# Ties between two queues: marks left by ScalarE instead of VectorE, and a fused mean subtraction in layernorm

## The chip, the cores and the metric

The kernel runs on one core of a Trainium2 chip. The metric is device time in microseconds. Three runs of the kernel before took 3631.34, 3631.67 and 3632.71 us; the median, 3631.67 us, is the time before. One more execution was taken with the hardware profiler on.

## The reference, cut to what matters

Sixteen graphs of 1024 nodes and 64 channels pass through four layers. Each layer starts with the same normalisation, and uses the adjacency matrix in its own way:

```python
def _layernorm(x, axis=-1, eps=1e-5):
    m = jnp.mean(x, axis=axis, keepdims=True)
    v = jnp.var(x, axis=axis, keepdims=True)
    return (x - m) / jnp.sqrt(v + eps)

# in each of the four layers
h = jnp.maximum(_layernorm(x, axis=-1), 0.0)
x = x + layer(h, adj)
```

- Layer 0 multiplies the adjacency with h (the messages), and puts h and the messages through two small matrices with a tanh between.
- Layer 1 is a weighted mean over neighbours: (A + I) h divided by the row sums.
- Layer 2 first drops some neighbours of nodes that have more than ten. For every node and channel it then sorts the values of the remaining neighbours and takes a weighted sum of their quartiles, which goes through two small matrices. This is where the gathers and sorts of the kernel come from.
- Layer 3 multiplies the adjacency with h once more, divides by the degree, and adds two small matrix products and a bias.

## The kernel before

**Engines and streams.** The kernel is one long program per engine, and each engine works through its own in order. The order is made when the program is written out. Six Python generators ("streams") each walk over the sixteen graphs: `adjacency` (load, transpose, which neighbours are dropped, keys), `layers` (layers 0 and 1 and the layernorm of layer 2), `tail` (the rest of layer 2, and layer 3), `gathers`, `neighbour_lists` and `sorts`. A loop at the end of `direct_path` always resumes the first stream in this list whose due time has come. Due times come from a small model, the object `clk`, with a planned time for VectorE (`clk.dve`), TensorE (`clk.pe`), ScalarE (`clk.act`) and GpSimd (`clk.pool`). A stream adds the planned cost of what it has issued, and yields the planned time at which it wants to go on. So a change of a planned cost can change the order of instructions, on VectorE above all.

`after(dve, pe, act, lat)` (line 824) is the helper with which a stream adds the planned costs of a step: VectorE's first, then TensorE's from there, then ScalarE's from there.

**Lists, gathers, sorts.** `neighbour_lists` finds each node's neighbours with repeated maxima over a row of keys (lines 1119 and 1133); the rows of keys are loaded by GpSimd with indirect transfers (line 1100, four buffers). Nodes are ordered by number of neighbours, and eight blocks of 128 nodes form five groups. For each group `gathers` has GpSimd issue one indirect transfer per neighbour place and block (line 1294: 124 of them per graph, 1984 in all), which fetch 128 rows of h into a buffer `raw`. Each group has one buffer, so its gathers for a graph follow its sort for the graph before. `sorts` runs a sorting network on VectorE (line 1327), then weighted sums (line 1346). The result is written out, and `tail` fetches it back in node order with eight more indirect transfers on GpSimd (line 1366). The planned cost of a gather is 1.39 us. A stretch of four gathers is issued when VectorE's planned time has come within 5 us of GpSimd's (`yield clk.pool - 5`).

**Ties.** At 35 places per graph (ahead of every stretch of gathers and once ahead of the key loads, 560 in all) the kernel calls `gate()` (line 920). If more than 3 us of VectorE's planned time have passed since the last one, VectorE writes one element of a tile `mark` (line 923; 8 slots in rotation, planned at 0.15 us), and GpSimd copies this element into a tile `gate` (line 925). The copied value is never used. The copy has to wait for VectorE's write, and everything behind it in GpSimd's order with it. The write of a slot has to wait for GpSimd's copy of eight marks before.

**Layernorm.** `preln` (line 849) runs four times per graph. VectorE sums each node's 64 channels (line 854), multiplies the sums by 1/64 (855), subtracts this from x by a broadcast (856); ScalarE squares (857); VectorE sums again (859); ScalarE takes the root (860); VectorE inverts and multiplies (862, 863); ScalarE applies the maximum with zero (864). In one of the four, x is read from PSUM.

**ScalarE around it.** In `layers`, TensorE's messages (line 883, 32 multiplications of 512 columns) are copied out by ScalarE (line 884). For layer 1, eight passes over the transposed adjacency follow on ScalarE, which give the degrees (line 1228). The step is accounted with

```python
        yield after(0, pe=14.0, act=1.1) + 6.0
        clk.act += 10
```

so that the planned time of the eight passes is added once the stream is resumed.

Of the kernel before, what the change touches and what calls it, by code (L numbers as in the profile page):

```python
# [7 lines left out]
F32 = mybir.dt.float32  # L8
# [6 lines left out]
ALU = mybir.AluOpType  # L15
AX = mybir.AxisListType

P = 128
C = 64
NB = 8  # L20
# [712 lines left out]
def direct_path(ctx: ExitStack, tc: tile.TileContext, t: dict, out: bass.AP, flag):  # L733
# [3 lines left out]
    nc = tc.nc  # L737
# [3 lines left out]
    const = ctx.enter_context(tc.tile_pool(name="const", bufs=1))  # L741
# [9 lines left out]
    tt, ts, act = nc.vector.tensor_tensor, nc.vector.tensor_scalar, nc.scalar.activation  # L751
# [13 lines left out]
    eps, none, wcol = cols[:, :1], cols[:, 1:3], cols[:, 3:6]  # L765
# [55 lines left out]

    clk = Clock()

    def after(dve=0.0, pe=0.0, act=0.0, lat=0.3):

        clk.dve += dve
        at = clk.dve
        if pe:
            clk.pe = at = max(clk.pe, at) + pe
        if act:  # L830
            clk.act = at = max(clk.act, at) + act
        return at + lat


# [10 lines left out]
    def mid(u, shape):  # L845

        return work.tile(shape, F32, tag=f"mid{u}", name="mid", bufs=2)

    def preln(u, x, ha):

        s = nodes.tile([P, 4, NB], F32, name="stat")
        xc = mid(u, [P, NB, C])
        sq = mid(u, [P, NB, C])
        nc.vector.tensor_reduce(s[:, 0], x, AX.X, ALU.add)
        ts(s[:, 1], s[:, 0], 1.0 / C, None, op0=ALU.mult)
        tt(xc, x, s[:, 1, :, None].to_broadcast([P, NB, C]), ALU.subtract)
        act(sq, xc, AF.Square)
        yield after(1.5, act=0.65, lat=1.2)
        nc.vector.tensor_reduce(s[:, 2], sq, AX.X, ALU.add)
        act(s[:, 3], s[:, 2], AF.Sqrt, bias=eps, scale=1.0 / C)  # L860
        yield after(0.7, act=1.0, lat=1.5)
        nc.vector.reciprocal(s[:, 2], s[:, 3])
        tt(xc, xc, s[:, 2, :, None].to_broadcast([P, NB, C]), ALU.mult)
        act(ha[:, :, :C], xc, AF.Relu)
        yield after(0.9, act=0.65)
# [45 lines left out]
    def even(v, u):  # L911

        return v.rearrange("c (q u p) -> c u q p", u=2, p=P)[:, u]


    marks = []
    slots = const.tile([1, 8], F32, name="mark")
    opened = const.tile([1, 2], F32, name="gate")

    def gate():  # L920
        if not marks or clk.dve > marks[-1] + 3.0:
            k = len(marks)
            nc.vector.memset(slots[:, k % 8:k % 8 + 1], 0.0)  # L923
            clk.dve += 0.15
            nc.gpsimd.tensor_copy(opened[:, k % 2:k % 2 + 1], slots[:, k % 8:k % 8 + 1])  # L925
            marks.append(clk.dve)


    state = [dict() for _ in range(B)]
# [161 lines left out]
    def neighbour_lists(b):  # L1091
# [5 lines left out]
        def load_keys(i):  # L1097
            if i < NB:
# [4 lines left out]
                ks.append((k, clk.pool + 3.5))  # L1103

        gate()
        for i in range(KB):
            load_keys(i)
# [84 lines left out]
    def layers(b):  # L1192
# [4 lines left out]
        yield max(g["at"], clk.dve + 3)  # L1197
        ha = nodes.tile([P, NB, C + 1], F32, name="ha")
        yield from preln(0, x, ha)
        zt = big(0, [P, N])  # L1200
        transposed(ha, zt[:C])
# [9 lines left out]
        yield after(0, pe=3.4, act=2.1) + 7.0  # L1211
        ha = nodes.tile([P, NB, C + 1], F32, name="ha")
        yield from preln(0, p, ha)

        nc.vector.memset(ha[:, :, C:], 1.0)  # L1215
# [25 lines left out]
        clk.dve += 1.6  # L1241
        ha = nodes.tile([P, NB, C], F32, name="h2", bufs=3)
        yield from preln(0, x, ha)
        nc.sync.dma_start(h_ds[b % 3][1:N + 1].rearrange("(i p) c -> p i c", p=P), ha)
        ts(deg[:, 1], deg[:, 0], 0.0, None, op0=ALU.is_equal)
# [9 lines left out]
    def gathers(b):  # L1255
# [4 lines left out]
        for k, (b0, n, cap, *_) in enumerate(GROUPS):  # L1260
# [13 lines left out]
            for s in range(cap):  # L1274
                if s % (4 // n) == 0 and s < PLACES[b0]:
                    gate()
                if k == 0 and s == 4:
                    for l, size in enumerate(sizes):
                        nc.gpsimd.indirect_dma_start(packed[:size, l * C:(l + 1) * C], None, h_ds[b % 3],
                                                     bass.IndirectOffsetOnAxis(ap=g["pack"][:size, l:l + 1], axis=0))  # L1280
                        clk.pool += 1.39
                if k == 0 and s == 11:
                    for l, size in enumerate(sizes):
                        nc.sync.dma_start(rows_d[l, :size], packed[:size, l * C:(l + 1) * C])
                if k == 0 and s == 17:
                    for l, p0, s0, ns, nn in PACKS:
                        nc.sync.dma_start(raw[:nn, s0:s0 + ns, :],
                                          rows_d[l, p0:p0 + ns * nn].rearrange("(n s) c -> n s c", s=ns))
                for i in range(n):
                    if s >= PLACES[b0 + i]:  # L1290
                        continue
                    clk.pool += 1.39
                    at = FIRST[k] + s * n + i
                    nc.gpsimd.indirect_dma_start(raw[:, s, i * C:(i + 1) * C], None, h_ds[b % 3],  # L1294
                                                 bass.IndirectOffsetOnAxis(ap=g["index"][:, at:at + 1], axis=0))
                if (s + 1) % (4 // n) == 0:
                    yield clk.pool - 5
# [189 lines left out]
@with_exitstack  # L1487
def kernel(ctx: ExitStack, tc: tile.TileContext, t: dict, out: bass.AP):
    nc = tc.nc
    pool = ctx.enter_context(tc.tile_pool(name="flag", bufs=1))  # L1490
    flag = pool.tile([1, 1], I32, name="flag")
    direct_path(tc, t, out, flag)
    many = nc.values_load(flag[:1, :1], min_val=0, max_val=P)
    with tc.If(many > 0):
        general_path(tc, t, out)
# [107 lines left out]
```

## Time and profile before

| | |
|---|---|
| median of three runs | 3631.67 us |
| profiled execution, its own time | 3640.35 us |
| its span, first to last instruction | 3638.5 us |
| mean granted TensorE clock | 0.698 |
| VectorE busy | 3072.9 us, 84% |
| GpSimd busy | 2651.7 us, 73% |
| TensorE busy | 1993.7 us, 55% |
| ScalarE busy | 1410.6 us, 39% |
| marks (line 923) | 462, of 59 ns |
| gates (line 925) | 462, 339 ns in the mean |
| scaled sums (line 855) | 64, of 182 ns |
| subtractions (line 856) | 64, of 692 ns |

In the profile PE is TensorE, DVE VectorE, ACT ScalarE, POOL GpSimd. A row of a group gives line, engine, operation, what it writes and reads, how often; then busy time and the mean of one; then the idle time of the engine just before such instructions, and what ended most of it. "issue" stands for idle time that no wait explains. A row of the waits gives total, number and longest. A row of the timeline gives start and length in us; an instruction may start before the one ahead of it has ended[...].[...]

### The profile page before, as it was taken

To read this page: it belongs to the slowest core of one execution; us is meant where nothing else is said; L and a number is where in the kernel's file an instruction comes from. 1 tells how busy PE (TensorE), PEld (TensorE's weight loads), DVE (VectorE), ACT (ScalarE), POOL (GpSimd) and SP (SyncE) were. 2 spreads that over 40 slices of the span, in tenths; PEclk is the share of its full clock that TensorE was granted. 3 is DMA by queue.
4 is the path that set the end of the run, shared out by engine and by line. 5 is a ranking of instruction groups with operands and counts; after the bars stand their busy time and mean duration, and the time that the engine had idled before them with its cause. 6 is when DMAs were issued, how large, how long until landed. Compare 5 with 4: busy or idle time off the path is not lost.

```text
span 3638.5 us, 31082 instructions
## 1 busy us (share of the span) xinstructions
PE 1993.7 (55%) x7587; PEld 923.9 (25%) x7587; DVE 3072.9 (84%) x7539; ACT 1410.6 (39%) x2770; POOL 2651.7 (73%) x2777
## 2 busy tenths in 40 slices
PE   6564565746666565746555556765646565550303
PEld 3222222323222222322222222232322322220101
DVE  3497989989898998989798997989898888989662
ACT  5444434344444344353444435443443534330000
POOL 1187787878777787877777787787778777777881
PEclk9676767676676676767676667667667776765555
DMA  2324243342424334151433425243332525232211
GB/s 90 120 62 122 60 129 102 112 129 62 152 66 133 95 109 128 49 184 44 145 81 111 122 72 166 55 134 89 126 109 63 167 56 157 49 123 52 74 27 57
DMA packets 237344, 362.38 MB, mean 100 GB/s; under 512 B 126848, under 2 KB 128496, under 8 KB 237152
## 3 DMA queue, kind: packets, MB, share of 16 engines
q1 hardware_dynamic: 156912, 255.00, 20.2%
q0 software_dynamic: 80096, 104.70, 14.1%
q8 instruction: 62, 1.02, 0.1%
q14 instruction: 130, 1.06, 0.1%
q10 hardware_dynamic: 144, 0.59, 0.0%
HBM read 245.30 MB, written 114.81 MB: 99 GB/s over the span
## 4 chain that ended last, share of the span: by engine, by line
DVE 61%; POOL 11%; issue 11%; DMA 7%; PE 5%; ACT 3%; SPq 0%; DVEq 0%; POOLq 0%; ACTq 0%
DVE raw L1327 16%; DVE other L1327 16%; POOL raw L1294 10%; DVE most L1133 6%; PE pt L883 4%; DVE found L1119 4%; DMA raw<-h_d,index 3%; DVE agg L1346 2%; ACT adjt L1228 2%; DMA k<-keys_d,node 2%; DVE k L1128 2%; DVE nb L948 2%; DVE found L1134 1%; DVE k L1130 1%; DVE gone L1007 1%
## 5 line engine op out<-in xcount | busy, mean ns | idle before, releaser
L1294 POOL DMA_INDIRECT raw<-h_d,index x1984 | 2165.2, 1091 | 558.8 <-issue 498.8
L1327 DVE TENSOR_TENSOR other<-raw 128x512 f32<-128x512 f32 (+11 forms) x816 | 536.4, 688 | 162.5 <-DMA raw<-h_d,index 132.9
L883 PE MATMUL pt<-adjt,ha 128*65 128x512 f32 (+1 forms) x1024 | 492.7, 643 | 91.0 <-DVE ha L1215 68.7
L995 PE MATMUL pt<-eh,nbt 128*128 128x512 f16 (+3 forms) x1024 | 236.6, 379 | 310.2 <-ACT nbt L984 309.7
L1327 DVE TENSOR_TENSOR raw<-other 128x512 f32<-128x512 f32 (+10 forms) x464 | 356.7, 791 | 5.6
L955 PE MATMUL pt<-ef,a 128*128 128x128 f32 x1024 | 205.2, 356 | 220.2 <-ACT adjt L957 136.2
L925 POOL COPY gate<-mark 1x1 f32<-1x1 f32 x462 | 156.4, 339 | 225.0 <-DVE mark L923 217.3
L1133 DVE MAX8 most<-k 128x8 uint16<-128x1024 uint16 x208 | 255.4, 1228 | 7.2
L962 ACT ACTIVATE nb<-nb 128x512 f16<-128x512 f16 x256 | 159.2, 624 | 255.6 <-DVE nb L948 149.6
L883 PEld LDWEIGHTS pt<-adjt,ha 128*65 128x65 f32 (+1 forms) x1024 | 149.9, 150 | 417.6 <-issue 403.3
L955 PEld LDWEIGHTS pt<-ef,a 128*128 128x128 f32 x1024 | 155.6, 183 | 321.6 <-ACT adjt L957 173.9
L995 PEld LDWEIGHTS <-nbt 128*128 128x128 f16 x1024 | 110.4, 120 | 436.0 <-ACT nbt L984 340.7
L1327 DVE TENSOR_TENSOR raw<-other,raw 128x640 f32<-128x640 f32 (+3 forms) x448 | 216.5, 494 | 5.0
L884 ACT COPY big<-pt 64x1024 f32<-64x1024 f32 (+1 forms) x32 | 32.3, 1008 | 476.8 <-PE pt L883 476.8
L1327 DVE TENSOR_TENSOR raw<-raw,other 128x128 f32<-128x128 f32 (+7 forms) x496 | 211.7, 436 | 6.0
L1403 PE MATMUL tm<-at,ha 128*64 128x512 f32 x512 | 175.3, 786 | 74.5 <-DMA at<-adjt_d 74.5
L1002 ACT ACTIVATE gone<-pt,sf 128x512 f16<-128x512 f32 x256 | 161.4, 683 | 124.5 <-DVE sf L976 95.3
L1029 PE MATMUL pt<-eh,gone 128*128 128x128 f16 x1024 | 127.2, 253 | 145.2 <-DVE gone L1007 77.8
L1327 DVE TENSOR_TENSOR other<-other,raw 128x128 f32<-128x128 f32 (+4 forms) x448 | 200.6, 459 | 3.8
L1119 DVE MAX8 found<-k 128x8 f32<-128x1024 f16 x128 | 156.3, 1221 | 51.6 <-DMA k<-keys_d,node 51.6
L891 PE MATMUL pt<-ef,res 128*128 128x128 f32 x128 | 38.9, 399 | 291.9 <-DMA res<-agg_d,pos 291.9
L1034 ACT ACTIVATE nb<-pt 128x1024 f16<-128x1024 f32 x120 | 122.4, 1020 | 164.9 <-PE pt L1032 89.2
(192 smaller groups left out, 4373.6 us busy)
## 6 DMA issues: line engine op xcount, KB each, us to landing
a<-in_adj_dram SPq DMA_DIRECT2D x64, 1024.0 KB
adjt_d<-adjt SPq DMA_DIRECT2D x64, 1024.0 KB
at<-adjt_d SPq DMA_DIRECT2D x128, 512.0 KB
keys_d<-nb SPq DMA_DIRECT2D x64, 512.0 KB
raw<-h_d,index POOLq DMA_INDIRECT x1984
x<-in_x_dram SPq DMA_DIRECT2D x16, 256.0 KB
h_d<-h SPq DMA_DIRECT2D x16, 256.0 KB
agg_d<-agg SPq DMA_DIRECT2D x16, 256.0 KB
```

The costliest lines, as they stand in the source:

```text
L883: nc.tensor.matmul(p[p0:p0 + n, s], h[:, j, :n], adjt[:, j, s], start=j == 0, stop=j == NB - 1)
L925: nc.gpsimd.tensor_copy(opened[:, k % 2:k % 2 + 1], slots[:, k % 8:k % 8 + 1])
L955: nc.tensor.transpose(p[:, u * P:(u + 1) * P], a[:, j * P:(j + 1) * P], identf)
L962: act(nb[:, i, s], nb[:, i, s], AF.Copy, accum_out=mn[:, q, i:i + 1])
L995: nc.tensor.matmul(p[:, o:e], nbt[:, j, :], stair[:, :e - o], start=j % 4 == 0, stop=j % 4 == 3 and j != i)
L1002: act(gone[:, i, s], p[:, s], AF.Abs, bias=sf[:, 2 + q, i:i + 1], scale=2.0)
L1029: nc.tensor.matmul(p[:, d], gone[:, j, i * P:(i + 1) * P], big_i, start=False, stop=j == 4 * q + 3 and i // 4 != q)
L1119: nc.vector.max(out=eights[0], in_=src)
L1133: nc.vector.max(out=most, in_=less.bitcast(U16))
L1294: nc.gpsimd.indirect_dma_start(raw[:, s, i * C:(i + 1) * C], None, h_ds[b % 3], bass.IndirectOffsetOnAxis(ap=g["index"][:, at:at + 1], axi ...
L1327: tt(view(two[to], *((i, vi) if greater else (j, vj)), w), view(two[s], i, vi, w), view(two[u], j, vj, w), ALU.max if greater else ALU.min)
L1403: nc.tensor.matmul(p[q * C:(q + 1) * C, :], ha[:, j, :], even(ats[j], q), start=j == 0, stop=j == NB - 1)
```

## The change

Two independent things are done.

First, the marks. ScalarE leaves them now, from inside `after`: whenever a step with ScalarE work is accounted and more than 3 us of ScalarE's planned time have passed since the last mark, ScalarE copies one constant element into one of 32 slots, and the mark is remembered with its planned time. `gate()` no longer makes a mark. It looks through the last 20 marks for those whose planned time is more than 1 us ahead of GpSimd's, takes the latest, and has GpSimd copy it, unless the last gate used the same one. VectorE's planned time no longer has the 0.15 us per mark; ScalarE's has 0.2 us per mark.

Second, the mean. The scaled sum of line 855 and the subtraction of line 856 become one operation, (sum x -1/64) + x, with the sum read by a broadcast.

```diff
     clk = Clock()
 
+    marks, gates = [], []
+    slots = const.tile([1, 32], F32, name="mark")
+    opened = const.tile([1, 2], F32, name="gate")
+
+    def mark():
+        if not marks or clk.act > marks[-1][0] + 3.0:
+            t = slots[:, len(marks) % 32:len(marks) % 32 + 1]
+            nc.scalar.copy(t, eps[:1])
+            clk.act += 0.2
+            marks.append((clk.act, t))
+
+    def gate():
+        due = [m for m in marks[-20:] if m[0] < clk.pool - 1.0]
+        if due and gates[-1:] != due[-1:]:
+            gates.append(due[-1])
+            nc.gpsimd.tensor_copy(opened[:, len(gates) % 2:len(gates) % 2 + 1], due[-1][1])
+
     def after(dve=0.0, pe=0.0, act=0.0, lat=0.3):
...
             clk.act = at = max(clk.act, at) + act
+            mark()
         return at + lat
...
         nc.vector.tensor_reduce(s[:, 0], x, AX.X, ALU.add)
-        ts(s[:, 1], s[:, 0], 1.0 / C, None, op0=ALU.mult)
-        tt(xc, x, s[:, 1, :, None].to_broadcast([P, NB, C]), ALU.subtract)
+        nc.vector.scalar_tensor_tensor(xc, s[:, 0, :, None].to_broadcast([P, NB, C]), -1.0 / C, x, op0=ALU.mult, op1=ALU.add)
         act(sq, xc, AF.Square)
...
-    marks = []
-    slots = const.tile([1, 8], F32, name="mark")
-    opened = const.tile([1, 2], F32, name="gate")
-
-    def gate():
-        if not marks or clk.dve > marks[-1] + 3.0:
-            k = len(marks)
-            nc.vector.memset(slots[:, k % 8:k % 8 + 1], 0.0)
-            clk.dve += 0.15
-            nc.gpsimd.tensor_copy(opened[:, k % 2:k % 2 + 1], slots[:, k % 8:k % 8 + 1])
-            marks.append(clk.dve)
```

## The prediction

> **What bounds the kernel now.** I read first the page's engine shares and the chain that ended last, then POOL's own groups in the stretch where it gathers (160 to 3560 us), then the waits.
>
> ```profile
> PE 1993.7 (55%) x7587; PEld 923.9 (25%) x7587; DVE 3072.9 (84%) x7539; ACT 1410.6 (39%) x2770; POOL 2651.7 (73%) x2777
> DVE 61%; POOL 11%; issue 11%; DMA 7%; PE 5%; ACT 3%; SPq 0%; DVEq 0%; POOLq 0%; ACTq 0%
> ```
>
> DVE looks like the bound and POOL like a second. The groups of POOL in the stretch 160 to 3560 us (count | busy us, mean ns | idle just before, and what ended it) say more:
>
> ```profile
> L1294 POOL DMA_INDIRECT raw<-h_d,index x1984 | 2165.2, 1091 | 558.8 <-issue 498.8 <-DVE mark L923 18.4 <-DVE raw L1327 10.7
> L925 POOL COPY gate<-mark 1x1 f32<-1x1 f32 x461 | 155.9, 338 | 96.0 <-DVE mark L923 88.3 <-DVE less L1143 4.1 <-DVE wts L1185 0.9
> ```
>
> With the three smaller groups busy time is 2627 us of 3400. The idle time before a gather is "issue", about 0.3 us ahead of each one, never absent (some 625 us over all groups), so POOL's own work is 2627 + 625 = 3252 us, and its true waits are 148 us, 96 of them at the gates. POOL is as good as full: it starts at 148 us, ends near 3550, and 85 us of tail follow. What POOL waits more or less in there can move the end. DVE is nearly full as well, and waits for POOL where the two meet:
>
> ```profile
> DVE other L1327 <- DMA raw<-h_d,index: 132.9, 20, 25.7
> DVE found L1119 <- DMA k<-keys_d,node: 51.6, 12, 11.2
> ```
>
> Taking for each group of gathers the end of its last gather and the start of the sort that uses it, the third and fourth groups of graphs 0 to 5, and the first group from graph 11 on, arrive just in time almost without exception (about 1 us either way of a landing 2 to 3 us after the last issue, the length of the 'DMA raw' pieces in the chain); the fifth has 30 to 45 us to spare in the first half. So a delay of POOL counts at those groups and is absorbed at the others.
>
> **What the Trainium skill says.** "Perfetto Trace Analysis", section Optimization Strategy, has one look for the gaps of the contended engine and what releases them; the above follows it. The same page, under DMA Instruction — SWDGE (GPSIMD), says that the profiled end of such a DMA is the end of descriptor writing, not the landing; the trace agrees, since DVE waits on 'DMA raw' after POOL has ended. "VectorE: DVE Perf Modes", section The TRN2 errata, gives a fp32 two-input operation of 512 elements 691 ns (the trace: 692 in line 856), and ScalarE 224 + elements cycles at 1.2 GHz from SBUF: 0.19 us for one element as an estimate. The trace has 243 ns for the 64-element copy in line 1269 (formula 240), and no one-element copy.
>
> **The change, part by part.**
>
> 1. Marks leave DVE: 462 memsets of 59 ns, 27 us busy. But they fill gaps. Timeline of DVE (start, us):
>
> ```profile
> 1402.68 0.69 DVE L948 TENSOR_SCALAR nb<-a 128x1024 f16<-128x1024 f32 x1
> 1403.40 0.23 DVE L950 TENSOR_TENSOR nb<-nb,eh 128x128 f16<-128x128 f16 x1
> 1403.55 0.54 DVE L1130 TENSOR_SCALAR k<-k,found 128x1024 int16<-128x1024 int16 x1
> 1403.57 0.06 DVE L923 MEMSET mark<- 1x1 f32 x1
> 1404.13 1.23 DVE L1133 MAX8 most<-k 128x8 uint16<-128x1024 uint16 x1
> ```
>
> The memset starts inside line 1130, and the maximum follows 0.58 us after 1130's start; without a mark (1400.70 to 1401.28 a moment earlier) it is 0.58 too. Over the 370 marks whose neighbours also occur without a mark, the median difference is 2 ns. So 462 x 2 ns = 1 us; the upper bound is 27. I take 1.
>
> 2. Mean: 64 of line 855 go, 64 fused operations take the place of 856. Line 1239, the same operation over 512 elements, takes 691 ns, 856 takes 692, from SBUF or PSUM: no difference. Line 855 to 856 start to start is 0.236 us in the mean, so DVE loses 64 x 0.236 = 15 us. With DVE on 61% of the chain: 9 us gained (0 if POOL sets the pace, 15 if DVE does).
>
> 3. POOL's gates. A gather follows a gather after 1.378 us, and after 1.597 with a gate between that doesn't wait: 0.22 us a gate. The plan's stamps are arithmetic in the code, so I laid the new rule on the stamps of the kernel before: 720 steps with ScalarE time give 502 marks; of 560 gate sites 363 find a mark that is new. 99 gates fewer x 0.22 = 22 us gained on the full engine. After 3200 us, 14 gates instead of 53.
>
> 4. ScalarE gets 502 copies of 0.19: 95 us busy, at 39% of the span. Behind each stands ScalarE's next operation. ScalarE is 3% of the chain: 95 x 3% = 3 us lost. If its idle time hid nothing the bound would be 95; if everything, 0. A mark can also wait for POOL to have read its slot, but 32 marks lie between, and POOL reaches a gate 2 to 10 us behind its mark in the trace: nothing.
>
> 5. Where the gates wait. Now a gate waits for a DVE memset that is put in DVE's order at that moment, with POOL's planned time up to 5 us later; that leaves 88 us of waits (and 129 us at the first gate, before any key exists; there the new rule sets no gate, since POOL's clock is still zero, and the key loads wait for their keys no shorter). After the change it waits for a ScalarE copy that was planned to end 1 us before POOL's planned time. The memset had nothing but DVE's order ahead of it; the copy stands behind everything in ScalarE's order, and ScalarE waits long for the message matmuls:
>
> ```profile
> 704.92 1.01 ACT L884 COPY big<-pt 65x1024 f32<-65x1024 f32 x1 [16.16 <-PE pt L883]
> 705.83 1.06 ACT L1228 ACTIVATE adjt<-adjt 128x1024 f32<-128x1024 f32 x1
> ...
> 714.07 0.19 ACT L1228 ACTIVATION_READ_ACCUMULATOR adjt<-adjt 128x1 f32 x1
> ```
>
> The step's DVE part is at 687.8. Its stamp is 14.0 (PE) + 1.1 (ScalarE) + 0.2 later, 703.1 in trace time, but the eight passes of line 1228 are in front of the mark and are counted only after it (clk.act += 10): the mark can start at 714.26, 11 us behind its stamp. POOL is then one gather short of a third group, and DVE waits for that one:
>
> ```profile
> 703.85 0.18 POOL L925 COPY gate<-mark 1x1 f32<-1x1 f32 x1
> 704.18 0.97 POOL L1294 DMA_INDIRECT raw<-h_d,index  x1 [0.16 <-issue]
> ...
> 707.17 2.36 DVE L1327 TENSOR_TENSOR other<-raw 128x1024 f32<-128x1024 f32 x2 [4.23 <-DMA raw<-h_d,index]
> ```
>
> This gate would take that mark: 10 us of wait, and DVE's 4.23 us become 14. Behind the gate in POOL's order stand that gather, the fourth group, then key loads and the tail's gathers; DVE's sorts and maxima wait for them. The step comes once per graph, and line 884 of layer 0 is like it. With the trace's times, 67 of the 363 gates find the mark not yet left: 302 us one by one (98 at line 1228, 62 at 884, 38 at 1059), against 85 for the old gates by the same reading (measured: 88). Since POOL, having waited, comes later to the next gate, they carry to 147 us: 147 - 88 = 59 us more. That is the term if each us more of wait costs a us. Below it lies the absorption by groups with time to spare, down to rival B. If DVE and ScalarE shift as a block each time a just-in-time group comes late, and make nothing good, the shifts add to 125 us more. I take 80, since DVE has other waits that shrink when it comes late.
>
> Sum: -1 -9 -22 +3 +80 = +51. The profiled execution spans 3638.5 us and took 3640.35; +51 is 3691. The median of the runs is 8.7 below the profiled execution, so 3683.
>
> **The rivals.**
>
> B, faster: gates that hold less. Marks are then older than POOL's arrival nearly everywhere, as they are for 296 of the 363 already. If waits at the gates fall from 88 to 40: -1 -9 -22 +3 -48 = -77, 3555 us; with none at all -117, 3515. For it: the 88 us of waits for DVE's marks all vanish, and the sorts that free a group's buffer and the lists that it needs are mostly done 30 us and more before its first gather, so nothing else holds POOL. Against it: the late marks of 1228 and 884 recur in every graph. It decides the sign where gate waits stay under 88 + 29 = 117 us.
>
> C, nothing: waits end near 117 us and pay back the saved work. 3632, within 7.3 us (0.2%, about what a measurement of this kernel can tell).
>
> D, much slower: a loop. A late gate delays the gathers, these the sort, DVE delays ScalarE's inputs, ScalarE the next mark. If all 32 late places cost their 10 us: 320 - 88 - 29 = +203, 3835 us. Against it: the slack of the fifth groups and of graphs 6 to 10 absorbs.
>
> The plan's DVE clock also loses 462 x 0.15 = 69 us, so DVE's order shifts. What this does I can't read from the trace; it may go either way by some 30 us, and is in the range.
>
> **How the numbers follow.** A, late marks, 0.62, with its own range 3645 to 3765; B 0.20; C 0.08; D 0.10. The prediction is A's 3683. The range reaches down to the nearer half of B, 3590, leaving out 0.10 of it, and up to 3775, leaving out 0.09 (most of D). Faster is B, 0.20; same C, 0.08; slower A and D, 0.72.
>
> **What would show it.** Right: POOL's gate rows wait on ScalarE's mark, above 117 us in total after the start, longest ones behind lines 1228 and 884; DVE's wait for 'DMA raw' grows from 133 to above 170; gates near 360, marks near 500, DVE's busy share in the steady part falls. Step 1 is right if DVE's time without waits drops by about 15 us and not 40. Wrong if the gate waits are under 90 us: then POOL runs on, the waits for raw shrink, and B holds. It would also be wrong if another order of the streams makes waits on keys or on the layernorm statistics grow or shrink by more than 30 us.

## The result and the profile after

The changed kernel takes 3660.70 us (median of four runs, 3657.18 to 3663.40), the kernel before 3632.19 us (four runs, 3631.34 to 3637.65). The ratio is 1.0076, with a 95% interval of 1.0063 to 1.0089: 28.5 us slower. The profiled execution took 3660.26 us and spans 3658.4. The lines of the code have moved: the mark is now line 832 on ScalarE, the gate 841, the gathers 1300, the sorts 1333, layernorm 874 to 881, the message copies 903, the eight degree passes 1234.

The page of the changed kernel, its engine shares and the head of its chain:

```profile
PE 2030.6 (56%) x7587; PEld 930.2 (25%) x7587; DVE 3066.2 (84%) x7013; ACT 1449.1 (40%) x3266; POOL 2614.3 (71%) x2682
...
DVE 53%; POOL 14%; PE 11%; DMA 7%; issue 7%; ACT 7%; DVEq 0%; SPq 0%; ACTq 0%; POOLq 0%
```

DVE has 526 instructions fewer and is busy only 6.7 us less. ACT has 496 more (the marks) and is busy 38.5 us more. DVE's share of the chain fell from 61 to 53%, ACT's rose from 3 to 7%, PE's from 5 to 11%.

POOL's groups between 160 and 3560 us:

```profile
L1300 POOL DMA_INDIRECT raw<-h_d,index x1977 | 2155.6, 1090 | 559.7 <-issue 526.6 <-ACT mark L832 11.0 <-DMA raw<-h_d,index 5.8
L841 POOL COPY gate<-mark 1x1 f32<-1x1 f32 x367 | 118.3, 322 | 121.7 <-ACT mark L832 101.3 <-ACT m L1088 12.1 <-ACT mv L1049 6.5
```

There are 367 gates in the place of 461, and they wait 121.7 us in the place of 96.0. DVE's waits (total, number, longest), those of before that the text below compares, and then those of after:

```profile
DVE stat L862 <- ACT stat L860: 48.3, 6, 18.1
...
DVE stat L859 <- ACT mid L857: 28.8, 6, 9.7
...
DVE pos L1062 <- ACT sink L1059: 19.3, 4, 10.5
...
DVE node L1085 <- ACT m L1082: 7.7, 2, 7.0
```

```profile
DVE other L1333 <- DMA raw<-h_d,index: 123.7, 23, 12.7
DVE found L1125 <- DMA k<-keys_d,node: 62.8, 17, 9.3
DVE stat L878 <- ACT mid L876: 39.2, 7, 11.7
DVE node L1091 <- ACT m L1088: 37.8, 4, 15.2
DVE pos L1068 <- ACT mark L832: 32.1, 4, 10.5
...
DVE stat L881 <- ACT stat L879: 16.9, 3, 13.1
```

The wait for gathered rows, 132.9 us before, did not grow: it is 123.7. What grew are waits for ScalarE: `node` on `m` was 7.7 us before, `pos` (on a mark that stands behind the `sink` passes) was 19.3 on `sink` itself, `stat` on `mid` 28.8. The wait of `stat` on ScalarE's root shrank from 48.3 to 16.9.

**An account in which every run can be read.** If all rows of DVE's waits are added up, the total is 457.3 us before and 486.3 after: 29.0 more. The span of the profiled executions grew by 19.9 us, since what DVE does outside its waits takes 9.1 less. (By the medians the time grew by 28.5 us; the profiled execution of the kernel before was 8.7 us longer than its median.) The same sum for the runs below, split by what ended the waits ("rows and keys" are the transfers that GpSimd issues):

| profiled execution | span | DVE's waits, all | rows and keys | ScalarE | TensorE | span less waits |
|---|---|---|---|---|---|---|
| before | 3638.5 | 457.3 | 184.5 | 134.7 | 84.2 | 3181.2 |
| mean alone | 3620.1 | 452.7 | 162.7 | 155.0 | 84.2 | 3167.4 |
| old order, new ties | 3599.6 | 431.8 | 151.1 | 160.6 | 84.2 | 3167.8 |
| new order, old ties | 3653.2 | 481.8 | 194.8 | 167.0 | 90.2 | 3171.4 |
| after | 3658.4 | 486.3 | 186.5 | 181.2 | 93.7 | 3172.1 |
| after, one true stamp | 3616.5 | 449.9 | 139.9 | 192.5 | 93.2 | 3166.6 |
| after, older marks | 3569.7 | 401.4 | 92.5 | 193.1 | 91.2 | 3168.3 |
| after, no gates | 3563.3 | 392.0 | 67.8 | 207.5 | 93.4 | 3171.3 |
| after, neither gates nor marks | 3587.1 | 420.2 | 80.3 | 220.4 | 90.7 | 3166.9 |
| after, once more | 3660.3 | 487.7 | 186.4 | 183.2 | 93.7 | 3172.6 |

(The rest of the waits, 23 to 54 us, are for loads and for "issue".) The last column is 3169.5 us within 3 us in every kernel with the fused mean, and about 12 more without it. So the fused mean takes some 12 us from what DVE itself does, and everything else acts through DVE's waits. The table says through which waits a kernel is longer; it doesn't say why they grew.

### The profile page after: what moved, and what is told of

Its sections match the earlier page's. It is cut to its first block, busy times and chain, and to the rows that moved or that the text cites. A ratio compares the mean times of both kernels' runs of the same rounds, so it can differ in the third digit from the quotient of the medians.

```text
span 3658.4 us, 30853 instructions
## 1 busy us (share of the span) xinstructions
PE 2030.6 (56%) x7587; PEld 930.2 (25%) x7587; DVE 3066.2 (84%) x7013; ACT 1449.1 (40%) x3266; POOL 2614.3 (71%) x2682
## 4 chain that ended last, share of the span: by engine, by line
DVE 53%; POOL 14%; PE 11%; DMA 7%; issue 7%; ACT 7%; DVEq 0%; SPq 0%; ACTq 0%; POOLq 0%
DVE other L1333 13%; DVE raw L1333 13%; POOL raw L1300 12%; PE pt L902 7%; DVE most L1139 6%; DVE found L1125 4%; ACT adjt L1234 3%; DMA k<-keys_d,node 3%; DMA raw<-h_d,index 2%; DVE agg L1352 2%; DVE k L1134 2%; DVE found L1140 1%; DVE nb L954 1%; DVE k L1136 1%; ACT sink L1065 1%
## 5 line engine op out<-in xcount | busy, mean ns | idle before, releaser
L1001 PE MATMUL pt<-eh,nbt 128*128 128x512 f16 (+3 forms) x1024 | 256.9, 404 | 353.9 <-ACT nbt L990 353.8
L1106 POOL DMA_INDIRECT k<-keys_d,node x128 | 130.7, 1021 | 190.3 <-DVE node L1091 128.1
L841 POOL COPY gate<-mark 1x1 f32<-1x1 f32 x367 | 118.3, 322 | 121.7 <-ACT mark L832 101.3
```

Source lines behind the costliest of these rows:

```text
L1001: nc.tensor.matmul(p[:, o:e], nbt[:, j, :], stair[:, :e - o], start=j % 4 == 0, stop=j % 4 == 3 and j != i)
L1106: nc.gpsimd.indirect_dma_start(k, None, g["keys_d"], bass.IndirectOffsetOnAxis(ap=g["node"][:, i:i + 1], axis=0))
```

## The experiments

All kernels compute the whole of the reference; the ties carry no data. Ratios and intervals are those on record, and can differ a little from the quotient of two medians. "Theory 1" in the expectations is that late marks cause the slowdown, "theory 2" that the new order does.

**The parts, in a slower series of runs.** The runs were made in three series. In that of the first four the kernel before itself took 3765.23 us (median of 34), so they are compared with that alone. Some expectations below speak of another chip. That isn't shown: the number of the chip was the same in this series and in the last one (the last four runs), in which the kernel before took 3631.90 us. What made the first series slower stays open.

The mean alone, on the kernel before:

```diff
-        ts(s[:, 1], s[:, 0], 1.0 / C, None, op0=ALU.mult)
-        tt(xc, x, s[:, 1, :, None].to_broadcast([P, NB, C]), ALU.subtract)
+        nc.vector.scalar_tensor_tensor(xc, s[:, 0, :, None].to_broadcast([P, NB, C]), -1.0 / C, x, op0=ALU.mult, op1=ALU.add)
```

> The kernel before with the fused mean subtraction alone; marks and gates stay on VectorE. Step 2 of the prediction: VectorE loses 15 us, of which 9 reach the end: 3622 us against 3632 (0 if GpSimd sets the pace, 3617 if VectorE does). No theory makes it slower.

Measured: 3785.38 us, 1.0049 [1.0029, 1.0070]: slower, which wasn't expected.

The marks alone, the diff of the change without its two lines on the mean:

```diff
             clk.act = at = max(clk.act, at) + act
+            mark()
```

> The changed kernel with the mean subtracted in two operations as before, so the marks' move alone. If the parts add up: the changed kernel's +28 us and the mean's 9 more, about 3670 us. If the mean is hidden: 3660.

Measured: 3839.21 us, 1.0199 [1.0157, 1.0242]. The gates' row in the stretch 160 to 3560 us:

```profile
L841 POOL COPY gate<-mark 1x1 f32<-1x1 f32 x363 | 114.8, 316 | 283.4 <-ACT mark L832 245.2 <-ACT mv L1050 15.3 <-ACT m L1089 11.9
```

The plan alone: the kernel before, with only a planned cost taken out. Every instruction stays; what changes is when the streams' turns come, and with that the order.

```diff
             nc.vector.memset(slots[:, k % 8:k % 8 + 1], 0.0)
-            clk.dve += 0.15
```

> The kernel before with its marks and gates where they were, but the planned 0.15 us per mark no longer added to VectorE's clock, as in the changed kernel. Theory 1, late ScalarE marks: the order of instructions matters little, 3622 to 3642 us. Theory 2, the plan: it is the lost 69 us of planned time that reorders VectorE's work, and the slowdown is here too: 3650 us or more.

Measured: 3795.57 us, 1.0074 [1.0050, 1.0099].

The changed kernel with that 0.15 us still charged to VectorE's planned time whenever the old rule would have made a mark:

```diff
+    ghosts = []
     def gate():
+        if not ghosts or clk.dve > ghosts[-1] + 3.0:
+            clk.dve += 0.15
+            ghosts.append(clk.dve)
         due = [m for m in marks[-20:] if m[0] < clk.pool - 1.0]
```

> The changed kernel, with the planned 0.15 us added to VectorE's clock at the places where a mark would have been made before, so that the plan is nearly that of the kernel before and the ties alone have changed (the fused mean is in). Theory 1: slow as the changed kernel or slower, 3655 to 3680 us, gate waits above 117 us. Theory 2: back to the time before less the mean's gain, 3620 to 3635.

Measured: 3837.24 us in the median of six, gate waits 284 us; the ratio, 1.0149 [1.0097, 1.0201], leaves out the longest of the six. This is what theory 1 expected. But the run doesn't separate what it was meant to: the 0.2 us per mark was still added to ScalarE's planned time, so the order was not that of before.

What follows from the four: removing a planned cost alone, without touching an instruction, made the kernel slower by 0.7% in this series. The sizes of the rest don't carry over to a series in which the kernel before takes 3632 us: the mean alone, which ran in both, has 210 us of gate waits here and 87 there, and is 0.5% slower here and 0.2% faster there.

**The gates' waits, and the gates.** Three edits of the changed kernel, and the changed kernel again. In the first a gate takes a mark at least 12 us old by the plan, in the second there is no gate (the marks stay), in the third there are no marks either (the diffs stand in this order; the third has the second's edit too).

```diff
-        due = [m for m in marks[-20:] if m[0] < clk.pool - 1.0]
+        due = [m for m in marks[-20:] if m[0] < clk.pool - 12.0]
```

> The changed kernel, but a gate takes the latest mark that was planned 12 us, not 1 us, ahead of GpSimd's time, so that marks are nearly always left when GpSimd comes; everything else, the plan too, is the same. Theory 1 (late marks hold the gathers): gate waits fall from 122 us to under 30, and the slowdown of 0.8% is gone, ratio to the kernel before 0.985 to 1.001. Theory 2 (the plan's changed order): the gate waits fall but the ratio stays above 1.005.

```diff
     def gate():
-        due = [m for m in marks[-20:] if m[0] < clk.pool - 1.0]
...
+        return
```

> The changed kernel with its marks on ScalarE, but no gate on GpSimd at all: gathers wait for their own data alone. Theory 1: GpSimd saves 367 gates of 0.22 us (80 us of work) and all gate waits, so clearly faster than before, ratio 0.96 to 0.99. If ties are needed to keep the gathers from colliding with something: not faster, ratio above 1.0. Theory 2: ratio near 1.0 or above, since the plan is as slow as the changed kernel's.

```diff
             clk.act = at = max(clk.act, at) + act
-            mark()
```

> As the run without gates, and without the marks too. Against it this tells the cost of 496 copies on ScalarE (and of their 0.2 us each in the plan). Prediction: 3 us, ratio lower by 0.001; at most 85 us if nothing hides them. Theory 3 (the copies delay ScalarE's chain, and so cause the slowdown): lower by 0.007 or more.

> The changed kernel once more, on the chip of these runs, as their measure. The first measurement gave a ratio of 1.0076. The chip of the first four runs was slower in all of them (the kernel before took 3765 us there); if this one is like it, the ratio lies nearer to 1.015 to 1.02, since its marks-only run had 1.020.

| against the kernel before, 3632.99 us | us | ratio | gates | their waits, 160 to 3560 us |
|---|---|---|---|---|
| older marks | 3578.64 | 0.9853 [0.9839, 0.9866] | 363 | 9.1 |
| no gates | 3562.37 | 0.9804 [0.9790, 0.9818] | 0 | none |
| neither gates nor marks | 3583.35 | 0.9863 [0.9848, 0.9878] | 0 | none |
| changed kernel again | 3658.66 | 1.0072 [1.0058, 1.0086] | 367 | 125.3 |

POOL's gates with the older marks, and its gathers and key loads without gates:

```profile
L841 POOL COPY gate<-mark 1x1 f32<-1x1 f32 x363 | 124.5, 343 | 9.1 <-ACT mark L832 7.4
```

```profile
L1297 POOL DMA_INDIRECT raw<-h_d,index x1984 | 2136.3, 1077 | 604.9 <-issue 586.3 <-DMA raw<-h_d,index 9.1 <-DVE raw L1330 3.7
L1103 POOL DMA_INDIRECT k<-keys_d,node x124 | 130.4, 1052 | 142.5 <-DVE node L1088 45.7 <-DVE found L1137 43.8 <-issue 21.0
```

With the older marks the order of all streams and nearly the number of gates are those of the changed kernel, and 116 us less of waits at the gates give 80 us: a microsecond of gate wait costs 0.7. This is what theory 1 expected; in this order, too, a kernel whose gates hardly wait is faster than the kernel before. The table above shows where it comes from and what is taken back: the waits for rows and keys fall by 94 us, those for ScalarE rise by 12. Without gates little else holds the gathers: what is not "issue" in their row is 19 us. But POOL then waits elsewhere. Its key loads have 142.5 us of idle time ahead of them (61.3 in the changed kernel), most of it for DVE, and the fetches of `tail` 115.1 (52.0). The kernel without gates is the fastest of all, 70.6 us under the kernel before. Taking the marks away as well was to gain a little and was worse by 21 us; there the planned 0.2 us per mark went too, so this is another order again, and not the price of a copy.

**Order against ties.** The two things that the change does to the ties (who leaves the mark and which mark is taken; what the plan is charged) can be crossed. "Order" means what both charges do together, VectorE's 0.15 us per mark taken out and ScalarE's 0.2 us put in. All four corners have the fused mean.

Old order with new ties: the changed kernel, ghosts of the old marks charged, ScalarE's marks not charged.

```diff
             nc.scalar.copy(t, eps[:1])
-            clk.act += 0.2
             marks.append((clk.act, t))
+    ghosts = []
     def gate():
+        if not ghosts or clk.dve > ghosts[-1] + 3.0:
+            clk.dve += 0.15
+            ghosts.append(clk.dve)
```

> The changed kernel's ties and fused mean, in the order of the kernel before: the planned 0.15 us per mark goes back on VectorE's clock, the 0.2 us does not go on ScalarE's. With the run of new order and old ties, the kernel before and the changed one it makes a square of order and ties. Theory 1 (late marks cause all of the slowdown): ratio 1.004 to 1.02, gate waits above 110 us. Theory 2 (the new order causes it): 0.990 to 1.002.

New order with old ties: VectorE leaves the mark at the gate again, by the old rule; the plan is charged as in the changed kernel.

```diff
-            nc.scalar.copy(t, eps[:1])
             clk.act += 0.2
...
+        if not gates or clk.dve > gates[-1] + 3.0:
+            k = len(gates)
+            nc.vector.memset(slots[:, k % 8:k % 8 + 1], 0.0)
+            nc.gpsimd.tensor_copy(opened[:, k % 2:k % 2 + 1], slots[:, k % 8:k % 8 + 1])
+            gates.append(clk.dve)
```

> The changed kernel's order and fused mean, but the marks left by VectorE and the gates where the kernel before has them. Theory 1: the old ties do no worse than before and the mean's gain shows: ratio 0.993 to 1.001. Theory 2: slow as the changed kernel, 1.005 to 1.012.

Old order with old ties is the mean alone once more:

> The fused mean alone once more, on a chip like that of the first measurement, if this is one. Step 2: 9 us of 3632 gained, ratio 0.9975; 1.000 if GpSimd sets the pace, 0.996 if VectorE does.

Measured, against the kernel before in the same series (3631.90 us):

| | old ties (VectorE) | new ties (ScalarE) |
|---|---|---|
| old order | 3623.70, 0.9977 [0.9971, 0.9984] | 3603.65, 0.9927 [0.9914, 0.9940] |
| new order | 3657.51, 1.0075 [1.0062, 1.0088] | 3658.66, 1.0072 [1.0058, 1.0086] (the changed kernel again, above) |

The traces bear out the two orders: marks and gates left aside, DVE, ACT and POOL each run the same instructions in the same sequence in both kernels of a row. The gates of the three new corners, in the stretch 160 to 3560 us, first old order and old ties, then old order and new ties, then new order and old ties:

```profile
L924 POOL COPY gate<-mark 1x1 f32<-1x1 f32 x461 | 155.5, 337 | 87.1 <-DVE mark L922 79.7 <-DVE less L1142 4.1 <-DVE wts L1184 0.6
```

```profile
L845 POOL COPY gate<-mark 1x1 f32<-1x1 f32 x374 | 113.3, 303 | 83.5 <-ACT mark L832 79.7 <-ACT m L1092 1.6 <-ACT mv L1053 0.6
```

```profile
L839 POOL COPY gate<-mark 1x1 f32<-1x1 f32 x461 | 160.1, 347 | 113.9 <-DVE mark L838 105.3 <-DVE less L1148 3.8 <-DVE den L1240 2.6
```

Read down a column: the order costs 34 us with the old ties and some 54 with the new. Read along a row: the new ties gain 20 us in the old order, and are the same within the intervals in the new one. The gates' waits go with the order, too: 87 and 84 us in the old, 114 and 125 in the new, whoever leaves the marks. So with ties that wait like these, the slowdown comes with the order that the plan writes and not with the engine that leaves the marks. The older marks above and the stamp below show the other half: in the new order the time is won back, and more, when the gates wait less. The old order without waits at its gates wasn't run.

A rival is TensorE's granted clock, 0.692 in the mean over the runs of the new order with old ties and 0.699 in the old. Over the 29 runs of the kernel before, the time is some 4 us longer for each 0.01 that the clock is lower; by this estimate 3 of the 34 us are the clock's. The kernel with one true stamp, below, has a low clock too (0.694) and takes 3619 us.

What the new order does to DVE is seen by the waits of the two corners with old ties. Old order:

```profile
DVE other L1326 <- DMA raw<-h_d,index: 121.7, 21, 13.5
DVE stat L861 <- ACT stat L859: 43.9, 6, 17.1
DVE found L1118 <- DMA k<-keys_d,node: 40.8, 12, 6.6
...
DVE pos L1061 <- ACT sink L1058: 20.0, 4, 10.6
DVE stat L858 <- ACT mid L856: 19.9, 3, 10.1
...
DVE node L1084 <- ACT m L1081: 7.9, 2, 7.3
```

New order:

```profile
DVE other L1332 <- DMA raw<-h_d,index: 142.4, 25, 22.7
DVE found L1124 <- DMA k<-keys_d,node: 52.4, 14, 9.5
DVE pos L1067 <- ACT sink L1064: 44.9, 7, 10.6
DVE stat L877 <- ACT mid L875: 38.6, 8, 11.4
DVE node L1090 <- ACT m L1087: 34.3, 4, 14.6
...
DVE stat L880 <- ACT stat L878: 16.2, 3, 12.4
```

DVE comes to `pos`, `node` and layernorm's second sum while ScalarE is still at work on what they read, and waits 70 us longer there; it waits 28 us less for layernorm's root, and 32 us longer for rows and keys, which POOL fetches (its gates wait 27 us longer). Smaller rows shrink. All together: 29 us more, for a span 33 us longer. Which of the exchanged turns does it was not taken apart.

**One true stamp.** The changed kernel, in its own order, with one mark per graph stamped 10 us later, which is what the plan gives the eight passes ahead of it (`after` hands `late` on to `mark`; it is 0 everywhere else); the plan's clocks aren't touched, only the rule by which a gate picks a mark.

```diff
-            marks.append((clk.act, t))
+            marks.append((clk.act, t, clk.act + late))
...
-        due = [m for m in marks[-20:] if m[0] < clk.pool - 1.0]
+        due = [m for m in marks[-20:] if m[2] < clk.pool - 1.0]
...
-        yield after(0, pe=14.0, act=1.1) + 6.0
+        yield after(0, pe=14.0, act=1.1, late=10.0) + 6.0
```

> The changed kernel, with one number changed: the mark left after the eight passes for the degrees counts as left 10 us later than the plan had it. The order of all instructions but the gates is the same. In the changed kernel 11 of 23 waiting gates and 90 of 119 us of gate waits stand behind this mark. Step 5 of the prediction: gate waits fall to about 30 us, and of the 80 us that the older marks gained, some three quarters are gained here too: ratio 0.988 to 0.995. If the late mark of this step is not the cause: 1.005 to 1.008.

Measured: 3619.17 us, 0.9968 [0.9957, 0.9978].

```profile
L841 POOL COPY gate<-mark 1x1 f32<-1x1 f32 x356 | 119.1, 335 | 83.8 <-ACT mark L832 80.2 <-ACT m L1088 2.1
```

Of this kernel's gate waits, those for a mark behind the degree passes fell from 90 to 6.6 us. But the total fell only from 121.7 to 83.8, not to the 30 that I expected: POOL comes earlier to the next gate, and finds the next late mark (34 us of waits are now behind the `sink` passes, line 1065). The ratio lies between the two that were expected, 0.988 to 0.995 if this mark is the cause and 1.005 to 1.008 if not. Still, 38 us less of waits gave some 40 us, more than the whole slowdown.

## Why the prediction was right or wrong

Forecast: 3683 us, slower; measured: 3660.7, slower, inside the likeliest case's own range. The steps ahead of the gate waits held, most by their size; the step that carried the sign did not. That the number came near is luck: the sum had no term for the order, and the +80 of its fifth step stood in its place.

**Step 1, memsets (-1): right.** They filled gaps. In the old order the span less waits is 3167.4 us with the memsets and 3167.8 without: 462 memsets of 59 ns are worth nothing that this account can show. The prediction's test was that DVE's time without waits falls by about 15 us and not 40; it fell by 9.1 in the changed kernel.

**Step 2, mean (-9): right.** In the last series the mean alone took 8.2 us off the median, an interval of 0.9971 to 0.9984; in that of the first four runs it was a loss of 0.5%, which the step has no room for. DVE's own time fell by 13.8 us; the step had 15 on DVE, of which 61% count.

**Step 3, fewer gates (-22): right where it could be seen alone.** 367 gates against a forecast 363, 496 marks against 502. In the old order the new ties saved 87 gates, by the step's price 87 x 0.22 = 19 us, with 3.6 us less of waits, and the time fell by 20.

**Step 4, the copies (+3): too small, as far as it can be told.** A copy took 173 ns; the Trainium skill's "VectorE: DVE Perf Modes", section The TRN2 errata, had led to 190. DVE's waits for ScalarE are 6 us longer with ScalarE's marks in the old order, 14 us in the new (table, third column from the right). That the copies are the cause is argued: no run leaves them out and keeps the order.

**Step 5, the gates' waits (+80): failed, in its size and as what sets the sign.** With the order held, the new ties moved the time by -20 us in the old order and by +1 in the new. Part of the mechanism is there as described. In the changed kernel 11 of the 23 waits at gates, 90 of 119 us, are for a mark behind the degree passes. POOL in the timeline, and ScalarE at that moment:

```profile
933.88 0.95 POOL L1300 DMA_INDIRECT raw<-h_d,index  x1 [0.31 <-issue]
950.39 0.18 POOL L841 COPY gate<-mark 1x1 f32<-1x1 f32 x1 [15.57 <-ACT mark L832]
951.05 1.22 POOL L1300 DMA_INDIRECT raw<-h_d,index  x1 [0.48 <-issue]
```

```profile
940.85 1.01 ACT L903 COPY big<-pt 65x1024 f32<-65x1024 f32 x1 [19.70 <-PE pt L902]
941.76 1.05 ACT L1234 ACTIVATE adjt<-adjt 128x1024 f32<-128x1024 f32 x1
...
949.04 1.05 ACT L1234 ACTIVATE adjt<-adjt 128x1024 f32<-128x1024 f32 x1
949.99 0.19 ACT L1234 ACTIVATION_READ_ACCUMULATOR adjt<-adjt 128x1 f32 x1
950.08 0.17 ACT L832 COPY mark<-cols 1x1 f32<-1x1 f32 x1
```

POOL ends a gather at 934.83 and stands until the mark at 950.08, 8.3 us of it for passes that the stamp doesn't know. This is the place that the step saw in the trace, and its 98 us one by one were near for the changed kernel; in the old order, for which they were worked out, the passes gave 53. Marks behind the message copies of layer 0, line 884 before, were to give 62 us and gave 1.2; those behind the passes of line 1059 (now 1065) were to give 38 and gave 5. So the 147 us of waits were too many: in the old order the new ties wait 83.5 us and gain. In the changed kernel waits rose by 26 us, and old marks in the new order wait 27 us longer too. DVE's wait for rows, which was to pass 170 us, fell to 124. That the late mark costs time is shown all the same: one true stamp gave some 40 us back. But it isn't what the new ties add to the old: in the new order the old ties were as slow, 3657.51 us against 3658.66.

**What took its place** is what the prediction left out of its sum: that VectorE's planned clock loses 69 us, "either way by some 30 us". The 0.2 us for each of 496 marks, which ScalarE's planned clock gains, changes the order too, and the prediction didn't weigh it; the crossed runs move both together. With the fused mean held fixed, the order is worth +34 us with the old ties. So the sum as measured is -8 for the mean, +34 for the order, and +1 for the new ties in that order, where 94 gates saved are paid back, as far as the table tells, in waits for ScalarE that are 14 us longer: +27, against 28.5 measured. These are steps from one kernel to the next, so they have to add up; taken the other way round they are -8 for the mean, -20 for the ties and some +54 for the order. The prediction's own last sentence names a sign by which this would show, waits on keys or on the layernorm statistics that change by more than 30 us: the wait for layernorm's root shrank by 31.4 us, which by these words speaks against the prediction, and all waits for ScalarE together grew by 46.

**The break-even.** The prediction put the point of no change at 117 us of gate waits, 29 above 88. But 88 is only what ended with a mark; the whole row was 96.0. Counted alike, the point lies at 125, and the 121.7 us measured would make the kernel 3 us faster. What the prediction had no term for are DVE's other waits: those for rows and keys, where gates show, are 2 us longer than before, those for ScalarE 46.

**The rivals.** B didn't come, and its figures for gates that don't hold were too low: it gave 3555 us for waits of 40 and 3515 for none; measured were 3579 for 9.1 us of waits and 3562 without gates. "Nothing else holds POOL" was wrong, as its key loads show, and DVE's waits for ScalarE are longer when POOL runs ahead (193 and 207 us against 181). C lay 28 us off. D's loop didn't come: 23 gates wait, not one in every late place.

**Open:** which exchanged turns cost the 34 us; how the 34 us divide between VectorE's planned clock and ScalarE's; whether the old order without gates would be faster still than 3562 us; what made the series of the first four runs slower, and why the fused mean alone lost time in it.

## What to carry to other kernels

Where a planner writes the order, an edit has two effects, what it does and what its planned cost does to everybody's turn; keep the old order with ghost charges, or keep the new order with the old instructions, before either is believed. A mark has to be stamped with all that stands ahead of it in its engine's queue, and one that is stamped too early stops another engine. And ask what a tie is for: here the kernel without gates was the fastest of those measured.

## What was not expected of the hardware

- 462 instructions of 59 ns cost VectorE nothing that shows: its span less its waits is 3167.4 us with them and 3167.8 without. Their planned 0.15 us each, taken out of the plan with no instruction changed, was worth 0.7% in the series of the first four runs.
- Series of runs differ. The kernel with the mean alone took 3785 us in the series of the first four runs and 3624 in the last, with gate waits of 210 and 87 us, and the fused mean itself was a loss in the one (1.0049) and a gain in the other (0.9977). The number of the chip was the same, so a difference between chips isn't shown.
- The nine profiles with the fused mean in the table split into a nearly constant part of DVE (3166.6 to 3172.6 us) and waits that take up the whole of the difference between 3563 and 3660 us, on an engine that the page calls 84 to 86% busy.
